# Attention's P·V product in column tiles of 32, with one copy out of PSUM, and new cost numbers for the planner

## The chip, the core and the metric

The kernel runs on one core of a Trainium2 chip. The metric is device time in microseconds from one launch; the figure of a kernel is the median of several runs. PE is TensorE, DVE is VectorE, ACT is ScalarE, POOL is GpSimd, and SP is the engine that issues DMAs.

## The reference

Two layers work on x, 128 sequences of 32 tokens with 256 features. Each layer adds three blocks to x, each behind a layer norm: a cross-attention to a context of 257 tokens per sequence, a self-attention, and a feed-forward block.

```python
x = x + _L0_xattn_ref(_layernorm(x), ctx_2048, ...)   # 16 heads of 16
x = x + _L0_attn_ref(_layernorm(x), ...)
x = x + _L0_ffn_ref(_layernorm(x), ...)
x = x + _L1_xattn_ref(_layernorm(x), mask, ctx_2048, ...)  # 32 heads of 8
x = x + _L1_attn_ref(_layernorm(x), ...)
x = x + _L1_ffn_ref(_layernorm(x), ...)               # 8 experts
```

The part that matters here is the attention over the context, in both layers:

```python
scores = jnp.einsum('bqhd,bkhd->bhqk', q, k) * scale
probs = jax.nn.softmax(scores, axis=-1)
out = jnp.einsum('bhqk,bkhd->bqhd', probs, v)
```

## The kernel before

The 128 sequences are handled in units of four, so there are 32 units per layer. Most products are made in float16 or bfloat16 with operands split into a high and a low half, so that one product takes three passes.

Attention over the context goes in steps, each a generator ("stream"). `ctx_gen` computes keys and values for all context tokens and writes them to DRAM; `load_k` and `load_v` fetch them. `rowpass` finds a row maximum per query and head. `pvpass` (line 813) takes each sequence b of a unit and each group of four blocks. A block is a set of four heads; with 32 queries each it makes 128 columns. For each of two chunks c of 128 context tokens it computes the scores of four blocks into one PSUM bank, lets ACT exponentiate them into P (128 tokens x 512) in `expP` (line 918), and lets POOL compute Pl, the low half, as P minus its bfloat16 top half. Then, one group later, `pv` (line 844) multiplies P by V and copies the product to Uc, from which `attn_fin` normalizes and projects.

In `pv` the 128x128 piece of P or Pl that belongs to a block is the stationary operand, and V of the block's four heads is the moving one. V holds for each head d low columns, d high columns and a column of ones (WS), where d is 16 in layer 0 and 8 in layer 1. The output is 128x68 for a block: rows are (head, query), columns are (head, 17). Only the four diagonal 32x17 pieces, where the row's head is the column's head, are wanted. Four copies on ACT (lines 863 to 866), one for each head's 32 partitions, pick them for four blocks at once, 32x68 each. Layer 0 has 128 calls of `pv` with 24 matmuls each, layer 1 has 256 calls with 16.

The order of work is planned in Python. `Est` (line 87) gives each instruction a cost (`cost`, line 137), places it on its engine in a gap that fits (`fit`, line 111), and follows data through `note` (line 179). `pipeline` (line 355) lets the stream with the earliest key take its next step, with a preference for streams of heavy matmul work when the tensor engine's clock is about to drop (`WARM`). At the end, lines 375 to 379 sort each engine's instructions by their estimated start and pin that order. PSUM is eight banks, taken by `tk` (line 330), which picks the one whose last use is estimated to end first. Every instruction is issued through the wrapper at line 234, so that all carry this line in the profile.

The lines of the planner's cost for ACT and POOL:

```python
if e == "act":
    return (50.0 if ins[0].space == PSUM else 92.0) + 93.0 * (len(ins) > 1) + 0.84 * m
if e == "pool":
    return 300.0 + 165.0 * n(o) if n(o) <= 8 else 149.0 + 2.1 * m
```

Of the kernel before, what the change touches and what calls it, by code (L numbers as in the profile page):

```python
# [17 lines left out]
PSUM = bass.MemoryType.PSUM  # L18
# [66 lines left out]


class Est:
    """Estimates when each instruction can run. It only decides the order in which units of work are emitted."""

    LAT = {"pe": 196.0, "act": 150.0, "dve": 135.0, "pool": 75.0, "dma": 910.0}  # L90

    def __init__(self):
        self.busy = {k: ([], []) for k in ("pe", "act", "dve", "pool", "hw", "dma")}
        self.w, self.r, self.free, self.slots, self.rec = {}, {}, {}, {}, []
        self.end = self.pe = 0.0
        self.cols, self.acc, self.prev, self.first, self.group = {}, {}, {}, {}, {}
        self.log = {k: [] for k in ("pe", "act", "dve", "pool", "dma")}

# [37 lines left out]
    @staticmethod  # L136
    def cost(e, op, outs, ins):
        def n(a):
            return math.prod(a.shape[1:])

        def half(a):
            return mybir.dt.size(a.dtype) == 2 and a.space != PSUM
        o = outs[0]
        if e == "pe":
            if op == "transpose":
                return max(25.0, n(o) / 2.4 * (2 if mybir.dt.size(ins[0].dtype) == 4 else 1))
            return 426.0 if mybir.dt.size(ins[0].dtype) == 4 else max(25.0, n(ins[1]) / 2.4 + 1.0)
        m = max([n(o)] + [n(a) for a in ins])
        if e == "act":
            return (50.0 if ins[0].space == PSUM else 92.0) + 93.0 * (len(ins) > 1) + 0.84 * m  # L150
        if e == "pool":
            return 300.0 + 165.0 * n(o) if n(o) <= 8 else 149.0 + 2.1 * m
        f = 1.0
        if op == "transpose":
            return 602.0
        if all(half(a) for a in [o] + [a for a in ins if n(a) > 1]):
            f = 0.5 if op == "tensor_tensor" else 0.3
        return 68.0 + 1.04 * m * f

    @staticmethod  # L160
    def region(a):
# [17 lines left out]
    def note(self, e, op, outs, ins, inst):  # L179
        t = 0.0  # L180
        R = [(a.tensor.name, self.region(a)) for a in ins]
        Wr = [(a.tensor.name, self.region(a)) for a in outs]
        for w, L in ((False, R), (True, Wr)):
            for n, (p0, p1, lo, hi) in L:
                t = max(t, self.first.get(n, 0.0), self.group.get(n, 0.0) if e == "pe" else 0.0)
                if w:
                    t = max(t, self.free.get(n, 0.0))
                    if n not in self.first:
                        t = max(t, self.first.get(self.prev.get(n), 0.0) + 1.0)
                for (q0, q1, l2, h2, wr), (end, by) in self.acc.get(n, {}).items():  # L190
                    if (w or wr or h2 == PSB) and q0 < p1 and p0 < q1 and l2 < hi and lo < h2:
                        t = max(t, end if (w or h2 == PSB) and by == e and e != "dma" else end + self.LAT[by])
        if e == "dma":
            t = self.fit("hw", t, 500.0)
            st = t - 500.0
            end = self.fit("dma", t + 650.0, math.prod(outs[0].shape) * mybir.dt.size(outs[0].dtype) / 360.0)
        else:
            d = self.cost(e, op, outs, ins)
            if e == "pe" and self.cols.get(int(t / TICK) - 1, 0.0) < WARM:
                d = max(25.0, 2.0 * d - 1.0)  # L200
            end = self.fit(e, t, d)
            st = end - d
            if e == "pe":
                k = int(end / TICK)
                self.cols[k] = self.cols.get(k, 0.0) + math.prod(ins[-1].shape[1:]) * ins[0].shape[0] / 128
                self.pe = max(self.pe, end)
                self.group[Wr[0][0]] = end
        self.log[e].append((st, len(self.log[e]), inst))
        for n, _ in Wr:
            self.first.setdefault(n, st)  # L210
        fin, end = end, end + self.LAT[e]
        for n, k in R:
            A = self.acc.setdefault(n, {})
            k += (False,)
            A[k] = max(A.get(k, (0.0, e)), (fin, e))
            self.r[n] = max(self.r.get(n, 0.0), end)
        for n, (p0, p1, lo, hi) in Wr:
            A = self.acc.setdefault(n, {})
            for k in [k for k in A if p0 <= k[0] and k[1] <= p1 and lo <= k[2] and k[3] <= hi]:
                del A[k]  # L220
            A[p0, p1, lo, hi, True] = (fin, e)
            self.w[n] = max(self.w.get(n, 0.0), end)
        self.end = max(self.end, end)
# [86 lines left out]
class Body:  # L310
# [287 lines left out]
    def ctx_v(self, n, t, ch, cl):  # L598
        nc = self.nc
        ps = self.tk()  # L600
        seq = [(x, b, k) for x, b in ((ch, 0), (ch, 1), (cl, 0)) for k in (0, 1)]
        for j in range(2):
            for i, (x, b, k) in enumerate(seq):
                nc.tensor.matmul(ps[:, j * 256:j * 256 + 256], x[:, k, t * 128:t * 128 + 128], self.W[f"wv{j}"][b][:, k, :], start=(i == 0), stop=(i == len(seq) - 1))
        for i in range(2):
            d = HD[i]
            vv = self.vv[i][self.vvi % 3]
            self.est.fresh(vv.tensor.name)
            v3 = vv.rearrange("p (b c) -> p b c", c=2 * d + 1)
            lo, hi = v3[:, :, :d], v3[:, :, d:2 * d]  # L610
            pv = ps[:, i * 256:i * 256 + 256].rearrange("p (b c) -> p b c", c=d)
            nc.scalar.copy(hi, pv)
            nc.vector.tensor_tensor(lo, pv, hi, ALU.subtract)
            nc.sync.dma_start(self.vd[i][n // 2][n % 2 * 4 + t], vv)
        self.vvi += 1
# [228 lines left out]
    def pv(self, u, p, b2, q2, layer, V, Ps, Uc):  # L844
        nc = self.nc
        d = HD[layer]
        nb = 64 // d
        yield [Ps[1][1]]
        po = self.tk()
        for i in range(4):  # L850
            blk = q2 * 4 + i
            o = po[:, i * 68:i * 68 + 68].rearrange("p (h c) -> p h c", h=4)
            for c in range(2):
                Ph, Pl = (x[:, i * 128:i * 128 + 128] for x in Ps[c])
                v = V[:, b2 * 2 + c].rearrange("p (a h c) -> p a h c", h=4, c=2 * d + 1)[:, blk]
                if layer:
                    nc.tensor.matmul(o, Ph, v, start=(c == 0), stop=False)
                    nc.tensor.matmul(o[:, :, d:], Pl, v[:, :, d:], start=False, stop=(c == 1))
                else:
                    nc.tensor.matmul(o, Ph, v[:, :, d:], start=(c == 0), stop=False)  # L860
                    nc.tensor.matmul(o[:, :, :d], Ph, v[:, :, :d], start=False, stop=False)
                    nc.tensor.matmul(o, Pl, v[:, :, d:], start=False, stop=(c == 1))
        for hh in range(4):
            r = slice(32 * hh, 32 * hh + 32)
            nc.scalar.copy(Uc[r, 2 * p + b2].rearrange("p (a c) -> p a c", c=17)[:, q2 * 4:q2 * 4 + 4],
                           po[r, :272].rearrange("p (a hh c) -> p hh a c", hh=4, c=17)[:, hh])
        if b2 and q2 == nb // 4 - 1:
            self.mark("pv", 2 * u + p)
        yield "pe"
# [803 lines left out]
```

## Time and profile before

| | |
|---|---|
| median of 3 runs | 3532.02 us (3527.23 to 3536.44) |
| profiled execution, span | 3532.9 us |
| mean granted tensor clock | 0.917 |
| HBM traffic | 318.82 MB read, 180.19 MB written |
| P, exponentials on ACT | x768, 438.4 us busy |
| Pl on POOL | x768, 813.6 us busy |
| V,P and V,Pl matmuls | x7168 |

The profiled execution's span, from its first to its last instruction, is 0.9 us longer than the median of the runs, so the two can be compared directly. "Busy" counts an engine's instructions from start to end, with overlaps counted once. A matmul's own length includes its way through the array, so that many overlap. A group line gives tiles written and read, shapes, the count, busy time and mean length, and then the engine's idle time before these instructions with what ended it.

### The profile page before, as it was taken

The page shows a single profiled execution, that of the slowest core. Times are in us where ns is not written, and L with a number is a line of the kernel's source. Part 1 is how long each engine was busy: PE and PEld are TensorE (multiplying, and loading weights), DVE is VectorE, ACT ScalarE, POOL GpSimd, SP SyncE. Part 2 cuts the span into 40 slices and gives each one's busy share as a digit, 9 for nine tenths or more (in the row PEclk, how much of TensorE's full clock was granted, in tenths as well). Part 3 has the DMA queues.
Part 4 walks back from the last instruction along what each step waited for, and adds up shares of the span by engine and source line. Part 5 has one row for each costly group of instructions (what it writes and reads, how often), then busy time and mean ns, then how long its engine had stood idle before and what let it go on. Part 6 is the DMA issues. An engine that isn't in the chain of part 4 may idle for free.

```text
span 3532.9 us, 95750 instructions
## 1 busy us (share of the span) xinstructions
PE 3027.0 (86%) x35473; PEld 2261.8 (64%) x35473; DVE 2868.5 (81%) x7365; ACT 2239.1 (63%) x6339; POOL 2020.9 (57%) x2313
## 2 busy tenths in 40 slices
PE   5889898898888899898776889989888898888888
PEld 2545666666666666665564677767676776766676
DVE  6888787788777887878777888879888888898876
ACT  3446666566666676675567766676676775766672
POOL 2445666666666676675564554555555655555562
PEclk9989999999999999998876899989898998989999
DMA  5646676666677677676546434454454544445420
GB/s 138 194 142 194 178 203 191 188 182 193 195 207 209 193 209 214 180 209 187 129 117 175 109 88 91 113 112 95 105 120 101 119 111 94 99 104 117 107 50 10
DMA packets 685970, 509.90 MB, mean 144 GB/s; under 512 B 226524, under 2 KB 673244, under 8 KB 685500
## 3 DMA queue, kind: packets, MB, share of 16 engines
q1 hardware_dynamic: 685500, 503.77, 54.2%
q8 instruction: 279, 4.57, 0.6%
q14 instruction: 191, 1.56, 0.2%
HBM read 318.82 MB, written 180.19 MB: 141 GB/s over the span
## 4 chain that ended last, share of the span: by engine, by line
DVE 18%; PE 16%; ACT 8%; DMA 5%; issue 2%; SPq 1%; POOL 1%; DVEq 0%; ACTq 0%; POOLq 0%
PE bank L234 16%; DVE mx L234 4%; DMA QstD<-ed 2%; ACT P L234 1%; ACT Uc L234 1%; DVE dS L234 1%; DVE xt L234 1%; SPq L234 1%; DVE eS L234 1%; DVE glu_t L234 1%; DVE fhid L234 1%; DVE lnh L234 1%; DVE rbt L234 1%; ACT Qb L234 1%; DVE s L234 1%
## 5 line engine op out<-in xcount | busy, mean ns | idle before, releaser
L234 POOL TENSOR_TENSOR Pl<-P 128x512 f16<-128x512 f32 x768 | 813.6, 1075 | 317.7 <-ACT P L234 313.5
L234 ACT ACTIVATE P<-bank 128x512 f32<-128x512 f32 x768 | 438.4, 600 | 114.8 <-PE bank L234 94.3
L234 DVE TENSOR_REDUCE mx<-bank 128x2 f32<-128x512 f32 x768 | 479.6, 681 | 7.9 <-PE bank L234 7.9
L234 ACT COPY Uc<-bank 32x68 f32<-32x68 f32 x1536 | 314.7, 205 | 159.9 <-PE bank L234 142.2
L234 ACT CAST vv<-bank 128x256 f16<-128x256 f32 x512 | 200.9, 403 | 251.5 <-DVE vv L234 119.6
L234 PE MATMUL bank<-V,P 128*128 128x68 f16 (+1 forms) x4096 | 304.6, 199 | 26.9 <-ACT P L234 16.6
L234 DVE TENSOR_TENSOR vv<-bank,vv 128x256 f16<-128x256 f32 x512 | 213.1, 423 | 122.9 <-ACT vv L234 115.3
L234 POOL TENSOR_TENSOR fhl<-fhid 128x256 f16<-128x256 f32 x256 | 156.7, 615 | 273.0 <-DVE fhid L234 229.6
L234 PE MATMUL bank<-V,Pl 128*128 128x36 f16 (+1 forms) x3072 | 290.7, 194 | 10.7 <-POOL Pl L234 10.6
L234 PEld LDWEIGHTS <-P 128*128 128x128 bf16 x4096 | 264.8, 102 | 42.4 <-issue 16.7
L234 PEld LDWEIGHTS <-Kst 97*128 97x128 f16 x4096 | 240.5, 102 | 76.2 <-issue 48.2
L234 PEld LDWEIGHTS <-Pl 128*128 128x128 f16 x3072 | 243.7, 100 | 41.9 <-POOL Pl L234 17.4
L234 ACT ACTIVATE glu_t<-bank 128x256 f32<-128x256 f32 x352 | 134.1, 383 | 172.3 <-PE bank L234 138.3
L234 PE MATMUL bank<-QstD,Kst 97*128 97x128 f16 x2048 | 207.0, 233 | 29.6 <-ACT P L234 9.5
L234 PEld LDWEIGHTS <-ch 128*128 128x128 f16 x2048 | 196.3, 100 | 54.8 <-issue 23.4
L234 POOL TENSOR_TENSOR kk<-kb,kk 128x512 f16<-128x512 f32 x128 | 147.1, 1167 | 111.0 <-ACT kk L234 110.8
L234 PEld LDWEIGHTS <-hT 128*128 128x128 f16 x1536 | 138.0, 103 | 113.3 <-issue 34.7
L234 PE MATMUL bank<-khf,eh 32*128 32x256 f16 (+1 forms) x1536 | 153.8, 296 | 56.8 <-DMA khf<-kd 13.7
L234 DVE SCALAR_TENSOR_TENSOR glu_t<-glu_t,bank 128x256 f32<-128x256 f32 x352 | 144.8, 411 | 68.6 <-ACT glu_t L234 67.3
L234 POOL TENSOR_TENSOR cl<-ct,ch 128x1024 f16<-128x1024 f32 x64 | 137.5, 2149 | 34.6 <-DMA xt<-in_x 22.5
L234 POOL TENSOR_TENSOR ss<-ss,sq 128x512 f32<-128x512 f32 (+1 forms) x65 | 82.7, 1272 | 120.9 <-ACT sq L234 72.9
L234 POOL TENSOR_TENSOR rbt<-rbt,rbt 128x512 f32<-128x512 f32 x64 | 83.0, 1297 | 100.9 <-DVE rbt L234 72.1
(470 smaller groups left out, 9459.5 us busy)
## 6 DMA issues: line engine op xcount, KB each, us to landing
Kst<-kd SPq DMA_DIRECT2D x384, 256.0 KB
kd<-kk SPq DMA_DIRECT2D x128, 512.0 KB
vd<-vv SPq DMA_DIRECT2D x256, 136.0 KB
V<-vd SPq DMA_DIRECT2D x64, 544.0 KB
vd<-vv SPq DMA_DIRECT2D x256, 132.0 KB
V<-vd SPq DMA_DIRECT2D x64, 528.0 KB
ct<-in_ctxm SPq DMA_DIRECT2D x64, 512.0 KB
khf<-kd SPq DMA_DIRECT2D x128, 256.0 KB
```

Of the source, the lines that this page charges most:

```text
L234: r = f(*a, **k)
```

## The change

In `pv`, each matmul over a whole block becomes four, one per head: the stationary operand is the 32 columns of P that belong to the head, the moving one is the head's 17 (16, 9) columns of V, and the output goes to the head's 32 partitions. The diagonal pieces of a block then lie in 17 columns of 128 partitions, and four blocks in 68 columns, which one copy brings to Uc. In layer 0 the order of the three passes stays; the columns of a pass are the same.

In `Est`, the cost function gets other numbers: for matmuls with 32 output rows, for ACT with two inputs, accumulated outputs or 32 or 64 partitions, for POOL and for some DVE operations; and `lock` moves a DVE instruction without PSUM operands past the end of the POOL instruction that is estimated to run at that time. These decide only the order of issue, for the whole kernel.

```diff
@@ class Est
+            if o.shape[0] == 32 and ins[0].shape[0] == 128:
+                return max(7.5, n(ins[1]) / 9.6 + 1.0)
...
-            return (50.0 if ins[0].space == PSUM else 92.0) + 93.0 * (len(ins) > 1) + 0.84 * m
+            ps = ins[0].space == PSUM
+            d = (50.0 if ps else 92.0) + (127.0 if ps else 93.0) * (len(ins) > 1) + 0.84 * m
+            return d + 100.0 * (len(outs) > 1) + 112.0 * (o.shape[0] in (32, 64))
         if e == "pool":
-            return 300.0 + 165.0 * n(o) if n(o) <= 8 else 149.0 + 2.1 * m
+            if n(o) <= 8:
+                return 350.0 + 160.0 * n(o)
+            d16 = mybir.dt.size(o.dtype) == 2
+            k = (1.665 if mybir.dt.size(ins[-1].dtype) == 2 and ins[-1].tensor.name == ins[0].tensor.name else 1.9) if d16 else 2.1
+            if any(a.ap[-1][0] == 0 for a in ins):
+                k = 1.68
+            return 147.0 + k * m
...
+        if op == "reciprocal":
+            f = 5.0
+        d = 58.0 * (op == "scalar_tensor_tensor" and len(ins) > 2)
+        if op == "tensor_copy" and ins[0].space == PSUM and o.shape[0] < 32:
+            f = 0.5
+        return 68.0 + d + 1.04 * m * f
+
+    def lock(self, t, op, outs, ins):
+        if not self.pl or any(a.space == PSUM for a in outs + ins) or op not in ("tensor_scalar", "tensor_copy", "tensor_tensor", "scalar_tensor_tensor"):
+            return t
+        i = bisect.bisect_right(self.pl, (t, 1e18)) - 1
+        return max(t, self.pl[i][1]) if i >= 0 else t
...
@@ def pv
-            o = po[:, i * 68:i * 68 + 68].rearrange("p (h c) -> p h c", h=4)
             for c in range(2):
...
                 if layer:
-                    nc.tensor.matmul(o, Ph, v, start=(c == 0), stop=False)
-                    nc.tensor.matmul(o[:, :, d:], Pl, v[:, :, d:], start=False, stop=(c == 1))
+                    seq = ((Ph, 0, 17, 0), (Pl, d, 17, d))
                 else:
-                    nc.tensor.matmul(o, Ph, v[:, :, d:], start=(c == 0), stop=False)
-                    nc.tensor.matmul(o[:, :, :d], Ph, v[:, :, :d], start=False, stop=False)
-                    nc.tensor.matmul(o, Pl, v[:, :, d:], start=False, stop=(c == 1))
-        for hh in range(4):
-            r = slice(32 * hh, 32 * hh + 32)
-            nc.scalar.copy(Uc[r, 2 * p + b2].rearrange("p (a c) -> p a c", c=17)[:, q2 * 4:q2 * 4 + 4],
-                           po[r, :272].rearrange("p (a hh c) -> p hh a c", hh=4, c=17)[:, hh])
+                    seq = ((Ph, d, 33, 0), (Ph, 0, d, 0), (Pl, d, 33, 0))
+                for k, (P, lo, hi, at) in enumerate(seq):
+                    for hh in range(4):
+                        r = slice(32 * hh, 32 * hh + 32)
+                        nc.tensor.matmul(po[r, i * 17 + at:i * 17 + at + hi - lo], P[:, r], v[:, hh, lo:hi],
+                                         start=(c == 0 and k == 0), stop=(c == 1 and k == len(seq) - 1))
+        nc.scalar.copy(Uc[:, 2 * p + b2, q2 * 68:q2 * 68 + 68], po[:, :68])
```

More of the change, by code (lines that the diff above doesn't have):

```diff
@@ L95, in __init__ @@
         self.end = self.pe = 0.0
+        self.pl = []
         self.cols, self.acc, self.prev, self.first, self.group = {}, {}, {}, {}, {}
@@ L146, in cost @@
                 return max(25.0, n(o) / 2.4 * (2 if mybir.dt.size(ins[0].dtype) == 4 else 1))
-            return 426.0 if mybir.dt.size(ins[0].dtype) == 4 else max(25.0, n(ins[1]) / 2.4 + 1.0)
+            if mybir.dt.size(ins[0].dtype) == 4:
+                return 426.0
+            if o.shape[0] == 32 and ins[0].shape[0] == 128:
+                return max(7.5, n(ins[1]) / 9.6 + 1.0)
+            return max(25.0, n(ins[1]) / 2.4 + 1.0)
         m = max([n(o)] + [n(a) for a in ins])
         if e == "act":
-            return (50.0 if ins[0].space == PSUM else 92.0) + 93.0 * (len(ins) > 1) + 0.84 * m
+            ps = ins[0].space == PSUM
+            d = (50.0 if ps else 92.0) + (127.0 if ps else 93.0) * (len(ins) > 1) + 0.84 * m
+            return d + 100.0 * (len(outs) > 1) + 112.0 * (o.shape[0] in (32, 64))
         if e == "pool":
-            return 300.0 + 165.0 * n(o) if n(o) <= 8 else 149.0 + 2.1 * m
+            if n(o) <= 8:
[5 more added lines that the diff above has]
+            return 147.0 + k * m
         f = 1.0
@@ L157, in cost @@
             f = 0.5 if op == "tensor_tensor" else 0.3
-        return 68.0 + 1.04 * m * f
+        if op == "reciprocal":
[9 more added lines that the diff above has]
+        return max(t, self.pl[i][1]) if i >= 0 else t
     @staticmethod
@@ L200, in note @@
                 d = max(25.0, 2.0 * d - 1.0)
+            if e == "dve":
+                t = self.lock(t, op, outs, ins)
             end = self.fit(e, t, d)
             st = end - d
+            if e == "pool":
+                bisect.insort(self.pl, (st, end))
+                if len(self.pl) > 4000:
+                    del self.pl[:1000]
             if e == "pe":
```

## The prediction

> **What bounds the kernel now.** I read the page's busy shares first, then busy time in three stretches of steady work, then the chain, then who waits for whom, and last single instructions in the timeline.
>
> ```profile
> PE 3027.0 (86%) x35473; PEld 2261.8 (64%) x35473; DVE 2868.5 (81%) x7365; ACT 2239.1 (63%) x6339; POOL 2020.9 (57%) x2313
> DVE 18%; PE 16%; ACT 8%; DMA 5%; issue 2%; SPq 1%; POOL 1%; DVEq 0%; ACTq 0%; POOLq 0%
> PE bank L234 16%; DVE mx L234 4%; DMA QstD<-ed 2%; ACT P L234 1%; ACT Uc L234 1%; DVE dS L234 1%; DVE xt L234 1%; SPq L234 1%; DVE eS L234 1%; DVE glu_t L234 1%; DVE fhid L234 1%; DVE lnh L234 1%; DVE rbt L234 1%; ACT Qb L234 1%; DVE s L234 1%
> ```
>
> No engine is full. The chain gives 51% of the span to named work (the rest is hand-over between engines): DVE 18, PE with its issue 18, ACT 8. In merged order of time the Uc copies hold 1.3% of it, 46 us.
>
> ```profile
> 800.00:1200.00 400.00, 353.40 (x3857) 251.65 (x3858) 309.56 (x793) 257.12 (x711) 260.78 (x270) 0.97 0.69 198
> 2600.00:3000.00 400.00, 350.73 (x4663) 280.52 (x4660) 343.99 (x885) 267.61 (x786) 223.80 (x287) 0.91 0.46 107
> ```
>
> Columns: window, its length, PE, PEld, DVE, ACT, POOL busy, granted clock, DMA share, GB/s. In layer 0 (first row) PE leads with 88%; in layer 1 PE and DVE are level at 88 and 86%, and the clock is lower. PE's busy includes the tail of each matmul: between starts, only about 70% of the span is columns being streamed, so PE also waits.
>
> ```profile
> L234 ACT COPY Uc<-bank 32x68 f32<-32x68 f32 x1536 | 314.7, 205 | 159.9 <-PE bank L234 142.2 <-DVE glu_t L234 0.5 <-DVE va L234 0.4
> L234 ACT CAST aTE<-bank 128x128 f16<-128x128 f32 x64 | 17.1, 268 | 15.1 <-PE bank L234 9.4 <-DVE aTE L234 3.8 <-DVE hT L234 1.2
> PE bank L234 <- ACT P L234: 43.7, 60, 2.8
> PE bank L234 <- ACT Uc L234: 26.1, 44, 1.6
> ```
>
> The first two are ACT groups (count, busy, mean ns), the last two PE's waits (total us, times, longest). All lines are 234, the helper that records every operation, so tiles identify the work.
>
> ```profile
> 2833.52 0.18 PE L234 MATMUL bank<-V,Pl 128*128 128x36 f16 x1
> 2833.55 0.19 PE L234 MATMUL bank<-V,P 128*128 128x68 f16 x1
> 2833.58 0.18 PE L234 MATMUL bank<-V,Pl 128*128 128x36 f16 x1
> 2833.69 0.37 PE L234 MATMUL bank<-ePT,Vb 128*64 128x32 f16 x12
> ...
> 3456.35 0.94 PE L234 MATMUL bank<-ePT,Vb 128*64 128x32 f16 x46
> ```
>
> A P·V matmul follows the last after 30 ns, though each lasts 180 to 190. Two things bear on the change. First, ePT·Vb uses 64 columns of the array and alternates between its halves: 46 of them start within 0.94-0.18 = 0.76 us, 17 ns each, so two halves work at once. Second, going from full width to 64 columns cost 0.11 us where 0.03 is usual. Over the trace, a change of the array's shape adds about 97 ns beyond the streamed columns (120 to 135 at half clock), in either direction.
>
> **The change, part by part.**
>
> *ACT copies.* 384 calls of pv (128 in layer 0, 256 in layer 1) each issue one copy instead of four. The four start 216 ns apart, so 864 ns a call, 332 us in all. One 128x68 copy isn't in the trace; as its bounds I take 107 ns (a 128-partition ACT instruction lets the next start about 105 ns before it ends, P starting every 477 for a length of 597) and 216 (68 columns as now; 64- and 128-partition copies of 128 columns last 259 and 268, so length hardly depends on partitions). With 160, ACT loses 384 x (864-160) = 270 us of occupancy. On the chain Uc is 46 us; removing 81% gives **-37 us**, bounds 0 and -80 (if the 26 us of PE waiting for Uc and part of the 44 for P, which queues behind Uc on ACT, go too). What is late next there is DVE, whose own work doesn't change.
>
> *P·V streaming.* Before: 3072 matmuls 32.3 ns apart in layer 0, 4096 at 28.3 in layer 1 (trace, full clock): 99+116 = 215 us, 30 ns each. After: 28672 matmuls, four for each old one. Here a rule speaks against the change: the Trainium skill, "TensorEngine Tiling (Array Packing)", section Performance Considerations, says each matmul has an overhead of about 60 cycles whatever its width, and not to tile along a dimension that is already small. This trace has such a floor: full-width matmuls with one column start 25 ns apart. By the rule, 28672 x 25 = 717 us, +502. The ePT·Vb row says otherwise: 17 ns a matmul with two tiles, 32 for the pair. Four quarter tiles then take between 18 ns (half the weight columns: 32 at 2.4 GHz is 13 ns, plus the 5 that the 64-column tile shows over its 27) and 32. I take 25, the trace's shortest repeat on one tile: 7168 x 25 = 179 us, **-36**; bounds -86 and +14 unless issue intervenes, see the rivals. The same number of columns is loaded and streamed in all.
>
> *Shape changes.* Before, P·V had the full array's shape like most of its neighbours. In the built programs' PE order I count 1218 changes of shape before and 2106 after: P·V goes in 520 pieces, bordered mostly by full-width work. 888 x 97 ns = **+87 us** of PE; bounds +60 (some hidden in a wait that exists anyway) and +115 (all at half clock). The same page, section Tiling Modes, says that a mode change drains the engine; the trace agrees, with a price.
>
> *The clock.* In the trace's 3.41 us steps, the clock of the next step is full where the columns streamed, weighted by the share of the array's rows and columns in use, exceed about 2740; this fits 97% of 1025 steps. [...] A P·V matmul in quarter width then counts a quarter. Reweighting today's P·V so, steps under the limit rise from 11.0 to 12.9% in layer 0 and 23.1 to 26.8% in layer 1: 28 more. A step near the limit has some 1.2 us of streaming, which doubles: **+33 us** of PE; bounds 0 (width not counted) and +60 (drains thin the activity too).
>
> *Est's costs.* They issue nothing, but each engine's order is pinned from them, so all orders are redrawn. Today Est gives a Uc copy 107 ns (216 real), Pl 1224 (998 between starts), a 32x128 ue copy 158 (279); after, Pl is 999 and ue 270. Today's plan thus misses 384 x 436 ns = 167 us of Uc and 31 of ue on ACT. Work which the plan doesn't know pushes later work off plan; with ACT's share of the named chain, 8/51, that is 198 x 0.16 = **-32 us**. DVE and POOL have the same work in another order, and SP's queue about as many transfers; I cost these at nothing, hidden by DMA shares of 0.46 to 0.69, but a redraw can land badly: bounds -100 and +60, an assumption no row bounds.
>
> *Sum.* PE gains -36+87+33 = +84 us. PE waits too, so not all of this is on the path: PE with issue has 18/51 = 35% of the named chain, giving +29. Span: 3532.9-37+29-32 = 3493. The span is 0.9 us above the median of the runs, so 3492 for the median; I say **3491**.
>
> **The rivals.**
>
> *Issue becomes the bound (slower).* The quarter tiles need eight PE instructions in 25 ns. The fastest long burst here is 46 pairs at 17 ns; nothing shows 64 or 96 pairs at 6. Suppose the first 46 of a call go at 6.25 ns and the rest at the floor of 25: a layer-1 call takes 288+18x25 = 738 ns (453 now), a layer-0 call 288+50x25 = 1538 (775): +73+98 = 171 us. With drains and clock +291, 35% of it +102, less 37 and no gain from the plan: 3597. It decides from a group of four above 41 ns: there PE's extra is 200 us and eats the 69 gained. For it: the floor of 25. Against it: adjacent tiles' starts 3 to 7 ns apart in ePT·Vb.
>
> *PE is the path (slower).* With 88% in both layers PE's +84 us pass whole, and ACT's relief ends in DVE's waits: +84-37 = +47, 3579. For it: the window rows. Against it: PE's idle time before matmuls, with waits on ACT, DVE and DMA.
>
> *Costs cancel.* Without a plan gain: -37+29 = -8, 3524; the bounds put this within no change.
>
> *The relief spreads (faster).* DVE waits for ACT (vv alone 115 us), PE for P; with groups at 18 ns and the plan's lower bound, -80+0-60 gives about 3393; I weigh it lightly.
>
> That the change doesn't do what it says is excluded by the built program: 384 copies of 128x68 and 28672 narrow matmuls are there.
>
> **How the numbers follow.** Likeliest case 0.45 (its own range 3450 to 3522: the bounds of ACT and streaming), cancelling 0.12, issue 0.2, PE as path 0.15, spread relief 0.08. Faster than 3521.4 by the 0.3% (11 us) that a measurement can tell from no change: 0.45+0.08 = 0.53. Same 0.12, slower 0.35. The range reaches into the fast and the issue case: 3415 to 3605.
>
> **What would show it.** Groups of four starting 18 to 32 ns apart confirm the streaming step; single starts of 25 ns the issue rival. Uc should show x384 with under 90 us busy, ACT near 57%. Gaps of about 0.1 us at both ends of a P·V piece confirm the drains, a granted clock of 0.90 overall (0.917 now) the weighting. If all these hold and the span still doesn't fall, the path shares or the plan's value were wrong.

## The result, and the profile after

The changed kernel takes 3625.2 us (median of 4 runs, 3622.74 to 3630.15) where the kernel before took 3530.57 beside it: a ratio of 1.0272, 95% interval 1.0257 to 1.0287. It is slower by 2.7%, outside the predicted range. The profiled execution spans 3628.4 us.

Busy shares, instruction fetches, the chain and two groups of the page of the changed kernel:

```profile
PE 3114.0 (86%) x56977; PEld 2277.5 (63%) x56977; DVE 2865.7 (79%) x7365; ACT 2003.1 (55%) x5187; POOL 2020.8 (56%) x2313
...
q8 instruction: 447, 7.32, 0.9%
...
PE 41%; DVE 30%; DMA 11%; issue 7%; ACT 7%; POOL 2%; SPq 2%; DVEq 0%; ACTq 0%; POOLq 0%
...
L264 PE MATMUL bank<-V,P 128*32 128x17 f16 (+1 forms) x16384 | 297.3, 177 | 64.9 <-issue 46.1
...
L264 ACT COPY Uc<-bank 128x68 f32<-128x68 f32 x384 | 82.4, 215 | 228.6 <-PE bank L264 225.8
```

ACT did what was planned: the copies went from 314.7 to 82.4 us. DVE and POOL are the same. Of the matmul group's 64.9 us of idle time, 46.1 end with "issue": the profile shows nothing that PE waited for. The chain of this page covers the whole span; the one of before does not, as the part on the prediction shows. PE's waits, first in the kernel before and then in the changed one (total us, times, longest):

```profile
PE bank L234 <- ACT Uc L234: 26.1, 44, 1.6
...
PE bank L234 <- issue: 8.3, 3, 3.7
```

```profile
PE bank L264 <- issue: 87.8, 54, 5.5
...
PE bank L264 <- ACT Uc L264: 5.4, 10, 1.5
```

The wait for Uc has fallen to a fifth, and the waits on issue have grown to ten times what they were. Of the changed kernel's 87.8 us, 76.9 lie in the first 1790 us, which hold layer 0's attention; of the 8.3 before, 4.6. Where they lie, the timeline of one layer-0 call shows (start us, length us):

```profile
903.33 0.25 PE L264 MATMUL bank<-V,P 128*32 128x17 f16 x8
903.39 0.20 PE L264 MATMUL bank<-V,Pl 128*32 128x17 f16 x3
906.89 0.20 PE L264 MATMUL bank<-V,Pl 128*32 128x17 f16 x1 [3.30 <-issue]
906.90 0.25 PE L264 MATMUL bank<-V,P 128*32 128x17 f16 x8
906.97 0.20 PE L264 MATMUL bank<-V,Pl 128*32 128x17 f16 x4
907.11 1.03 PE L264 MATMUL bank<-wbh,hT 128*128 128x512 f16 x2
```

PE stops 3.3 us in the middle of four equal matmuls, between the third and the fourth, with all data long there. The instruction queue, q8, explains it. It brings 16 KB records (7.32 MB in 447), 256 instructions of 64 bytes each; PE's loads and matmuls, 113954, make 445 such blocks. On the page of before:

```profile
q8 instruction: 279, 4.57, 0.6%
```

The record that ends this stop starts at 904.56 us and lands at 905.48, and PE goes on 1.41 us later. In the changed kernel I count 35 stops longer than 0.5 us inside P·V at an instruction that waits for no semaphore: each ends 1.23 to 1.62 us after such a record landed (median 1.43). They also lie at one place of a block. Numbered along everything that PE's queue executed (loads, matmuls, its own semaphore instructions), the matmul that had to wait is number 193 or 194 modulo 256 in all 35. Of all of PE's waits on issue, those at numbers 193 to 195 make 84.3 of 87.8 us in the changed kernel and 0.0 of 8.3 us in the kernel before, where the three matmuls concerned do wait for semaphores.

Fetches never start closer than 3.4 us in this trace: 256 / 3.4 is 75 instructions a microsecond, the most that it shows. Full-width P·V takes a load and a matmul each 30 ns, 67 a microsecond, just below this; quarter tiles take them each 7.5 ns, 267. Before, the two closest fetches start 4.56 us apart; after, 105 follow within 5 us of the last. This is the window of the stop (PE, PEld, DVE, ACT, POOL busy; clock; DMA share; GB/s):

```profile
903.40:906.90 3.50, 0.20 (x26) 0.11 (x15) 1.44 (x3) 0.89 (x2) 2.26 (x2) 0.50 1.11 301
```

The stop did not lower the clock: the granted clock is 0.50 from 902.32 us, before the stop, to 912.56. The DMA engines are full in this window. No run varied that traffic, but the trace bears on it. I took the 129 blocks before whose fetch PE was running fast, and measured to the start of the fetch from the instruction that lies 300 ahead of the block's first one, the earliest at which any fetch of these two kernels starts. The median is 1.13 us where the DMA engines were less than 40% busy meanwhile (53 blocks) and 2.49 us where they were full (31); in layer 0 alone 1.16 and 2.72. The record itself takes 1.09 and 1.26 us. So full DMA engines go with a fetch that starts later; that they cause it is not shown.

**Theories.** Supply: the calls of layer 0 outrun the instruction fetch, and PE stands. Rivals: the drains, that is, the gap at each of 900 more changes of the array's shape; the redrawn order.

### The profile page after: what moved, and what is told of

It reads as the page before. It is cut to its first block, busy times and chain, and to the rows that moved or that the text cites. A ratio compares the mean times of both kernels' runs of the same rounds, so it can differ in the third digit from the quotient of the medians.

```text
span 3628.4 us, 137606 instructions
## 1 busy us (share of the span) xinstructions
PE 3114.0 (86%) x56977; PEld 2277.5 (63%) x56977; DVE 2865.7 (79%) x7365; ACT 2003.1 (55%) x5187; POOL 2020.8 (56%) x2313
## 3 DMA queue, kind: packets, MB, share of 16 engines
q8 instruction: 447, 7.32, 0.9%
## 4 chain that ended last, share of the span: by engine, by line
PE 41%; DVE 30%; DMA 11%; issue 7%; ACT 7%; POOL 2%; SPq 2%; DVEq 0%; ACTq 0%; POOLq 0%
PE bank L264 41%; DVE mx L264 6%; SPq L264 2%; DMA QstD<-ed 2%; DVE eS L264 1%; DMA khf<-kd 1%; DMA QstA<-e2d 1%; DVE vv L264 1%; DVE bS L264 1%; DVE lnh L264 1%; DVE xt L264 1%; DVE dS L264 1%; DVE glu_t L264 1%; ACT vv L264 1%; DVE fhid L264 1%
## 5 line engine op out<-in xcount | busy, mean ns | idle before, releaser
L264 PE MATMUL bank<-V,P 128*32 128x17 f16 (+1 forms) x16384 | 297.3, 177 | 64.9 <-issue 46.1
L264 PEld LDWEIGHTS <-P 128*32 128x32 bf16 x16384 | 250.6, 95 | 141.2 <-issue 125.7
L264 PE MATMUL bank<-V,Pl 128*32 128x9 f16 (+1 forms) x12288 | 285.9, 173 | 31.8 <-issue 22.7
L264 PEld LDWEIGHTS <-Pl 128*32 128x32 f16 x12288 | 245.2, 95 | 62.6 <-issue 40.6
L264 PE MATMUL bank<-khf,eh 32*128 32x256 f16 (+1 forms) x1536 | 165.9, 305 | 83.8 <-DMA khf<-kd 29.0
L264 ACT COPY Uc<-bank 128x68 f32<-128x68 f32 x384 | 82.4, 215 | 228.6 <-PE bank L264 225.8
L264 PEld LDWEIGHTS <-eh 32*128 32x128 f16 (+1 forms) x1536 | 49.4, 96 | 164.3 <-issue 137.7
```

The lines of the kernel that those rows point to most:

```text
L264: r = f(*a, **k)
```

## The experiments

Times differ between chips by 0.3%, so all figures are ratios to the kernel before on the same chip. "New planner" is the changed cost function.

**1. The planner alone.** The class `Est` of the changed kernel, `pv` as before.

> The new planner numbers alone, with the old P.V (full-width matmuls, four copies). Supply theory (the changed kernel loses its time where PE waits for instructions in layer 0): the planner is nearly innocent, 3500 to 3540, no waits of PE on issue above 10 us. Order theory (the redrawn order costs the time): 3580 or more. The prediction's own term was -32, 3498.

Measured: 3554.58 us, ratio 1.0044 (1.0028 to 1.006); waits on issue 7.7 us. The supply theory's range was overshot by 0.4%; the prediction's -32 us had the wrong sign, at least in this draw of the order (see 7).

**2. The new P·V alone.** The `pv` of the changed kernel, `Est` as before.

> The new P.V alone, planned with the old numbers. Supply theory: 3600 to 3640, with 60 to 110 us of PE waiting on issue. Order theory: below 3580. 2131 changes of array shape against 1218 before, 43000 more PE instructions.

Measured: 3890.96 us, 1.0996 (1.0966 to 1.1025), with 68.3 us on issue. No theory expected 10%; supply gave the waits, but not the time. Run 6 takes it up.

**3. One layer each.** `pv` chooses by layer between old and new body.

```diff
+        yield from (self.pv1 if layer else self.pv0)(u, p, b2, q2, layer, V, Ps, Uc)
```

> Quarter tiles and one copy in layer 0 only, layer 1 as before, new planner numbers. Changes of shape 1532 (+270 against the new planner alone), PE instructions +18400. Supply theory: nearly the whole loss is here, 3590 to 3625, PE waiting on issue 60 to 90 us. Drain theory (each change of shape passes its 97 ns to the span): +26 us, 3540 to 3560.

> Quarter tiles and one copy in layer 1 only, layer 0 as before, new planner numbers. Changes of shape 1810 (+548), PE instructions +24600, in calls of 128 instructions instead of 192. Supply theory: 3520 to 3550, PE waiting on issue under 25 us. Drain theory: +53 us, 3580 to 3600.

Measured: layer 0 alone 3606.57 us, 1.0176 (1.0147 to 1.0206); layer 1 alone 3558.0, 1.0051 (1.0033 to 1.007), which is the new planner's own level. PE's waits on issue, in layer 0 alone and in layer 1 alone:

```profile
PE bank L264 <- issue: 78.3, 39, 4.6
```

```profile
PE bank L264 <- issue: 16.4, 13, 4.5
```

Layer 1 has twice as many of the new changes of shape and a third more new instructions, yet costs nothing on balance; the stops and the loss are in layer 0. A call there is 192 instructions instead of 128, the matmuls around it belong to the context's keys and values, and the DMA engines are busier: 0.64 of the time in a stretch of layer 0 of the changed kernel (800 to 1200 us), 0.45 in one of layer 1 (2600 to 3000). Which of these makes the difference is not separated. All of it speaks for supply and against drains. Over the new planner alone the two layers cost 1.3 and 0.1 points, the two together 2.3; the missing 0.9 is not accounted for and lies within the scatter of run 7.

**4. Fewer instructions, same changes of shape.** Half tiles, and merging two passes of layer 0. The kernel with half tiles copies only one head's columns of each pair and so leaves out half of the product.

```diff
-                    for hh in range(4):
-                        r = slice(32 * hh, 32 * hh + 32)
+                    for hh in range(2):
+                        r = slice(64 * hh, 64 * hh + 64)
...
```

> P.V by two 64-column tiles for two heads each, one 128x68 copy, new planner numbers. It copies only the columns of each pair's first head, so half of the product is left out; matmul columns are 34 instead of 17. Changes of shape stay (2053), PE instructions fall to 82700 (111400 in the changed kernel, 68300 before); a layer-0 call takes 96 instructions in 24 pairs of tiles. Supply theory: PE waits on issue under 20 us, 3530 to 3565. Drain theory: as the changed kernel, 3610 to 3630.

```diff
-                    seq = ((Ph, d, 33, 0), (Ph, 0, d, 0), (Pl, d, 33, 0))
+                seq = ((Ph, 0, w, 0), (Pl, d, w, d))    # w = 2 * d + 1 columns per block in Uc
```

> Quarter tiles, but in layer 0 the two passes with P become one with 33 columns, the low and high columns stay apart in Uc and POOL adds them once more per unit. A layer-0 call takes 128 PE instructions instead of 192 (103200 in all, 8200 fewer than the changed kernel), changes of shape stay (2093). Supply theory: stalls on issue fall by half or more, 3570 to 3595. Drain theory: 3615 to 3630.

Measured: half tiles 3553.03 us, 1.0033 (1.0018 to 1.0049); merged 3575.99, 1.0101 (1.0076 to 1.0126). PE's waits on issue, half tiles first:

```profile
PE bank L264 <- issue: 8.3, 5, 3.8
```

```profile
PE bank L264 <- issue: 43.6, 27, 5.6
```

Both lie in the range that supply gave and far from that of the drains: with 2053 changes of shape but calls of 96 instructions, stops and loss are gone; with 128 in layer 0, half the stops stay. Layer 1's calls also have 128 and hardly stop (16.4 us in all in run 3), so the length of a call is not all of it.

**5. Drains alone, and density alone.** Three kernels with full-width P·V and extra matmuls whose output is not used; `Pd` is `Ps[0][0]`.

```diff
+        nc.tensor.matmul(po[:32, 480:497], Pd[:, :32], V[:, 0, :17], start=True, stop=True)   # drains: at both ends of a call
+        for g in range(0 if layer else 24):                                                   # dose_wide
+            nc.tensor.matmul(po[:, 300:368], Ps[0][0][:, :128], V[:, 0, :68], start=True, stop=True)
+        for g in range(0 if layer else 24):                                                   # dose_narrow
+            for hh in range(4):
+                r = slice(32 * hh, 32 * hh + 32)
+                nc.tensor.matmul(po[r, 300:317], Ps[0][0][:, r], V[:, 0, :17], start=True, stop=True)
```

> Old P.V under the new planner, with one extra 32-column matmul of 17 columns at the start and one at the end of each call, into unused columns of the same bank. 768 more matmuls, 2583 changes of shape against 1262 with the new planner alone: +1321, x 97 ns = 128 us of PE. Supply theory: no stalls on issue; the drains pass in part, +30 to +60 on the new planner alone. Drain theory: they pass whole, +110 to +130.

> Old P.V under the new planner, with 24 extra full-width matmuls of 68 columns at the start of each layer-0 call into unused columns of the bank: 128 x 24 x 30 ns = 92 us of PE, 6144 more PE instructions, no new changes of shape. Supply theory and its rival (what costs is the array's time and its drains): a part of the 92 passes, +15 to +45 on the new planner alone, PE waiting on issue under 20 us.

> As the wide dose, but each extra matmul is cut into four quarter tiles of 17 columns: the same 0.72 us of array time per layer-0 call in four times the instructions (24600 more than the new planner alone), and 290 more changes of shape (28 us of PE, of which the drain run let a fifth through). Supply theory: 30 to 90 us slower than the wide dose, with 50 us or more of PE waiting on issue. Rival (array time and drains only): within 15 us of the wide dose, waits on issue under 20 us.

Measured: drains 3578.77 us, 1.0112 (1.0092 to 1.0132), 0.68% or 24 us above the new planner alone for 1321 changes of shape, 18 ns each where PE itself loses 97. The scatter of run 7 is larger than these 24 us, so they only show that the drains don't pass whole (128 us would be 3.6%). Wide dose 3570.85, 1.0102 (1.0072 to 1.0131); narrow dose 3679.05, 1.0416 (1.0392 to 1.0441). First the group of extra matmuls and PE's wait on issue in the wide dose, then both in the narrow one (the wide group holds 3072 P·V matmuls too):

```profile
L264 PE MATMUL bank<-V,P 128*128 128x68 f16 x6144 | 400.5, 198 | 23.4 <-ACT P L264 7.2 <-DVE mx L264 4.9 <-DVE xt L264 2.6
```

```profile
PE bank L264 <- issue: 4.1, 3, 2.4
```

```profile
L264 PE MATMUL bank<-V,P 128*32 128x17 f16 x12288 | 130.5, 176 | 35.7 <-issue 34.1 <-DVE kk L264 0.7 <-DMA VL<-vld 0.6
```

```profile
PE bank L264 <- issue: 72.1, 48, 4.8
```

This is the price by itself. The same 68 columns in four instruction pairs instead of one cost 3.1%, 111 us, over the wide dose, more than the 30 to 90 expected, and the stops come with them: 72.1 us against 4.1. Of the remaining 43 us, 290 further changes of shape explain 5 at 18 ns each; the rest is not accounted for and about as large as the scatter of run 7.

**6. What the old planner lacked.** New P·V, old numbers, with only the matmul's new cost.

```diff
+            if o.shape[0] == 32 and ins[0].shape[0] == 128:
+                return max(7.5, n(ins[1]) / 9.6 + 1.0)
```

> New P.V, old planner numbers with one exception: the new cost of a matmul with 32 output rows (7.5 ns). Without it the old planner books 25 ns for each of 28672 matmuls, 717 us of PE where 215 are used, and the run was 10% slower than before. If that booking is the cause, this takes 3600 to 3660 (the changed kernel's level); if some other cost number is, it stays above 3750.

> A try at a version that is faster than before: quarter tiles and one copy in layer 1 only (calls of 128 PE instructions), full width and four copies in layer 0, old planner numbers plus the 7.5 ns for matmuls with 32 output rows. Under the new planner numbers the same kernel equals the new planner alone. Supply theory: 0 to +0.5% against the kernel before; if the ACT time that it frees is worth what the prediction booked, -0.5 to -1%.

Measured: 3643.25 us, 1.0319 (1.0292 to 1.0347), so this one number takes back 6.8 of run 2's 10%. The planner that books 25 ns for a 7.5 ns matmul plans 500 us of PE work that doesn't exist, and the pinned order is bad by 240 us. The version for layer 1 alone with these numbers was to be a better kernel, and isn't: 3594.95, 1.0159 (1.0132 to 1.0185), beyond both expectations. It has 16.8 us of waits on issue, no more than under the new planner at 1.0051. The 1.1 points between the two are within the scatter of run 7; why this order is worse stays open.

**7. The scatter of the order.** One planner latency moved by 5 ns: the same instructions in another order.

```diff
-    LAT = {"pe": 196.0, "act": 150.0, "dve": 135.0, "pool": 75.0, "dma": 910.0}
+    LAT = {"pe": 196.0, "act": 155.0, "dve": 135.0, "pool": 75.0, "dma": 910.0}
```

> The kernel before, with one planner latency (ACT) 155 ns instead of 150: the same instructions in a slightly other order. It measures what a redraw of the order does by itself. If the new planner's +0.4% is no more than such a redraw, this differs from before by 0.2 to 0.6% in either direction; if the order is robust, by less than 0.1%, and the +0.4% is the new numbers' own.

> The changed kernel with one planner latency (ACT) 155 instead of 150 ns: same instructions, other order. Supply theory: +1.8 to +3.2% against before, with 60 us or more of PE waiting on issue. Luck-of-the-order theory: it lands within 0.8% of before.

> The changed kernel with the same planner latency at 145 ns. As for 155: supply theory +1.8 to +3.2% and 60 us or more on issue; luck-of-the-order theory within 0.8% of before.

> The new planner alone (old P.V) with that latency at 155 ns. With its +0.44% and the +0.7% of the redrawn kernel before, 0 to +1% is expected, and no stalls on issue; above 1.5% would say that the order is most of the loss.

Measured: the kernel before, redrawn, 1.007 (1.0049 to 1.0091); the changed kernel 1.0215 (1.0188 to 1.0241) and 1.0219 (1.0192 to 1.0246), with 88.6 and 81.2 us on issue; the new planner alone 0.9917 (0.9892 to 0.9942), 3507.03 us. That last one is below what was expected and faster than both kernels, by nothing but its order. It has 16.1 us of waits on issue, where none were expected; none of them is at a block's border, and its matmuls wait for semaphores. All six kernels without bursts of smaller tiles have 0.0 us at the borders; half tiles have 1.0, and the kernels with quarter tiles 9.2 (layer 1 alone, run 6) to 84.3. So wide P·V lies at 1, 1.007, 1.0044, 0.9917, and quarter tiles in both layers under the new planner at 1.0272, 1.0215, 1.0219 (1.0319 in run 6). The two don't overlap. Under the new planner the means are 0.998 and 1.0235: the new P·V costs 2.5%, 90 us, and the planner's +0.4% is inside the scatter.

**8. Pacing.** Layer 0's call in two halves, the bank held between them.

```diff
+            if i == 2 and not layer:
+                yield "pe"
```

> The changed kernel with each layer-0 call of P.V split in two halves of 96 PE instructions, between which the planner may put other work; same instructions, 2213 changes of shape instead of 2106. Density theory: waits of PE on issue fall from 88 to under 60 us and the time falls by 10 to 50 us against the changed kernel. Number theory: waits and time stay, or the time grows by the extra drains (up to 10 us).

Measured: 3640.23 us, 1.0288 (1.0256 to 1.0321), waits on issue 64.1 us. A quarter of the waiting went, a little less than density would have, and no time with it. In layer 0 the trace has 151 pieces of half a call and still 25 of a whole one, and between neighbouring half pieces lie 33 PE instructions in the median; a stretch then outruns 256 instructions as before. This run decides nothing between density and number, and it shows, with run 6 (42.6 us of waits at 1.0319), that time does not follow these waits one for one. That instructions run out is shown; how much of the 2.5% each stop makes is not.

## Why the prediction was wrong

*Streaming, the step "I take 25 ... unless issue intervenes".* The rate of the tiles came inside my bounds: four quarter tiles take 30 to 31 ns (7.5 ns from start to start in layer 1 and 7.7 in layer 0), and the rule of 25 ns for each matmul that I set aside did not hold. But 30 is what one wide matmul took before, so the -36 us were nothing. The exception is where the step failed. I put waiting for instructions at nothing, looked for issue as a longer step from one matmul to the next, and set "a group of four above 41 ns" as the point from which it decides. Groups stayed at 30 and the loss came all the same, because instructions run out in blocks: full speed, then 0.5 to 5.5 us of nothing, 84 us in all. The rival "Issue becomes the bound" named the side and nearly the size, 3597, through a mechanism that isn't there; that it came near is luck. The trace of before held half of the right one: 279 blocks of 256 instructions, never less than 4.56 us apart (56 a microsecond), to set against eight in 30 ns (267). It did not hold the limit, since no stretch of it ran dry. The Trainium skill, "Runtime: NRT & Kernel Launch", section Instruction fetch mechanics, describes the refill in blocks of 256 instructions, as seen here, and calls its cost mostly hidden; here some 80 us of it are not.

*PE's share of 35%.* The chain on the page of before does not cover the span. It begins at 1744.6 us, where layer 0's attention is over but for its end; that is why its shares sum to 51%, and what I took for hand-over between the engines is the first half, in which nothing was followed. So 8/51, 18/51 and the 46 us of Uc tell of the second half alone. The kernel before, redrawn in run 7, has a whole chain:

```profile
DVE 34%; PE 33%; ACT 12%; DMA 11%; issue 6%; SPq 2%; POOL 2%; DVEq 0%; ACTq 0%; POOLq 0%
```

PE with issue is 39% there, so that 35 was near it by luck. The share was meant for work beside other work. A stop in the middle of a call holds back everything queued behind it on PE, in a stage where PE leads. Layer 0's last score matmul moved from 1692 to 1774 us, 82 us, against 72 us of new stops in that layer.

*ACT, -37.* One copy lasts 215 ns, the upper bound, and ACT lost 236 us of busy time where 270 us of occupancy were forecast. (The lower bound was mis-worked: 597 less 477 is 120 ns, not 105.) The value was not seen: layer 1 alone took two thirds of the relief and changed nothing against the new planner alone. What it gained and what its 548 drains cost can't be told apart there.

*Drains, +87 of PE.* 2151 changes of shape in the trace, each with its gap, as counted. In the drain run 18 ns of 97 passed to the span, but one draw of the order carries that figure and the scatter is larger.

*Clock, +33.* I named 0.90 as the sign of the column weighting and 0.902 came. But the new planner alone, with wide P·V, has 0.901. The sign proves nothing. The trace after speaks against the weighting. In its 3.41 us steps I compared two counts with the same limit of 2740: columns weighted by rows alone, and by rows and columns. Of the 222 steps in which quarter tiles make over a fifth of the count, the first tells the next step's clock rightly in 93%, the second in 86%; of the 36 steps where they differ, 26 are followed by full clock. In the trace of before both are right in 97% of the steps, which is why it could not decide.

*Planner, -32.* A misfit of planned and real ACT time turned into a gain by a share of the chain: no run supports this. Two draws of the new planner gave +0.4 and -0.8%. My bounds of -100 and +60 were fair, the central value was not knowledge. (The last rival's 3393 takes -60 for the plan where this lower bound is -100.) It also hid that an order redrawn for any reason moves the time by more than the 0.3% that I called no change.

*The rival "PE is the path"* saw rightly that delays of PE pass whole in layer 0, and came to 3579, but with drains and clock as the cause; layer 1 alone, with 548 drains and no loss, contradicts that.

## What to carry to other kernels

Before splitting an instruction into several that run side by side, compare the instructions per microsecond of a whole call with what the instruction queue has ever delivered, besides the engine's time: the engine's own rate can be right and the stream still dry. Places where the DMA engines are full deserve the first look. Where a planner pins the order, a wrong cost for one frequent instruction can cost more than the change itself (6.8% here against 2.5%), and a difference below the scatter of redrawn orders (1.5% from lowest to highest here) says nothing about a change until it has been redrawn once or twice.

## What the hardware showed that I had not expected

PE's instructions arrive in 16 KB blocks, never closer than 3.27 us in any of these traces, and a PE that ran dry in P·V resumes 1.2 to 1.8 us after a block lands, always at the same place of a block. With the DMA engines full a fetch starts more than 1 us later than with them less than 40% busy (2.49 against 1.13 us). Quarter tiles of the array, loads included, do run at 7.5 ns from start to start for dozens of pairs. A change of the array's shape costs PE 97 ns; in the one run that isolates it 18 of them reached the span, a figure below the scatter of the order.
